# Two-layer attention kernel on one core: a group's scores in two stretches instead of four, the first behind the weighting

## The chip, the cores and the metric

The kernel runs on one core of a Trainium2 chip. A core has five engines with a queue each, which work in order and wait for one another by semaphores: TensorE (PE, with its weight loads as PEld), VectorE (DVE), ScalarE (ACT), GpSimd (POOL) and SyncE (SP), which here only issues DMAs. Matmuls write to PSUM, eight banks of 128 x 512 fp32. The metric is the device time of one execution in microseconds (us); less is better.

## What is computed

The reference has two layers over x of shape 8 x 512 x 256. Layer 1 is, for each of the 8 batches, causal attention with 16 heads of 64 and rotary embedding, beside an 8-bit quantised product; layer 2 (a gated attention and a token-mixing network) is not touched by the change. Cut to what matters:

```python
xn = layernorm(x)                                  # B, S, D = 8, 512, 256
q, k, v = (xn @ W + b for W, b in ((Wq, bq), (Wk, bk), (Wv, bv)))   # 16 heads of 64
q, k = rope(q), rope(k)
scores = where(causal, q @ k.T / 8, -1e9)          # per head, 512 x 512
x = x + softmax(scores) @ v @ Wo + bo + int8_product(xn)
```

All of it is fp32, but for the quantised product.

## The kernel before

**Groups.** The heads of a batch are taken eight at a time, so layer 1 is 16 groups, numbered `at` = 0 to 15 (`last`); `b, g = divmod(at, 2)` gives the batch and its half. A group has two pairs of four heads, 2at and 2at + 1. Its steps, each a function of the kernel:

- `project_qk(pair, which)` (L387): four matmuls (L400; each fp32 matmul shows as two passes in the trace) make queries (`which` 0) or keys (1) of four heads; ScalarE takes them out of PSUM with the bias (L405), and SP sends them off with partitions exchanged (`y`, L407). `project(at, which)` does both pairs.
- `turn_qk(pair, which)` (L410): the rotary embedding, two VectorE products (L417) and one sum on GpSimd (L432).
- `project_v(at)` (L434): the values, taken out by ScalarE (L449) and stored; `load_v` (L455) fetches them back in another layout (`vr`, one buffer).
- `scores(at, run)` (L469): the causal scores in blocks of 32 queries. The 16 blocks are packed into nine units of one pair of PSUM banks each, and the units into five runs (two units each, the fifth has one). Every unit takes two banks; matmuls are 64 rows by 32 columns, eight side by side in the array (L480).
- `soften(at, run)` (L487): VectorE adds the mask, finds the maximum and writes the scores to SBUF (`p`, L508, four buffers), ScalarE exponentiates with the sum (L512).
- `divide(at, run)` (L518): reciprocal on VectorE (L523), multiplication by it on GpSimd (L531), an instruction for each block and half.
- `turn(at, run)` (L539): VectorE transposes the probabilities in 32 x 32 blocks (L551) into `turned`, four tiles with one buffer each.
- `weigh(at)` (L560): probabilities times values, 256 matmul passes of 32 rows by 64 columns (L568) into four banks. Its first matmul reads a tile that all five runs write, `turn(at, 4)` last. `keep_weighed` (L576) takes them out on ScalarE (L582).
- `output_product` and `add_output` (L356, L368; together `finish`): the output projection (L362) and its addition on VectorE (L371).

`look_at(b)` (L291; statistics on VectorE, L152 to L156, and a small power on GpSimd, L157) and `prepare(b)` (L305; normalisation, L171, and the greatest value, L301) make a later batch's input ready, in the groups with `g == 1` and 1 <= b < 6 and in group 2; `transpose_x` (L312) turns it on TensorE in groups with `g == 0`. The groups 12 and 13 also round and clip an input (L190, L196) and add the quantised product of a batch (`add_quantised`, L199).

**Order.** The tile scheduler is switched off (`manual_schedule`, L256), so each engine's queue has exactly the order in which the program calls these functions; the loop at L813 is that order, written by hand. PSUM has one pool of eight banks in rotation (`bank`, L60): a new tile waits for the readers of the tile eight allocations before it. In the loop of group `at`, TensorE's order is scores 0 of `at`, the weighting of `at - 1`, scores 1, the queries of `at + 1`, scores 2, the values of `at + 1`, scores 3 and 4, the output product of `at - 1`, and the keys of `at + 2`.

## Time and profile before

| | |
|---|---|
| median of 3 runs | 941.17 us (938.4 to 942.62) |
| the profiled execution | 939.1 us, its span 937.2 us |
| PE busy | 923.8 us, 99% of the span |
| DVE busy | 787.4 us, 84% |
| ACT busy | 533.0 us, 57% |
| POOL busy | 540.0 us, 58% |
| granted TensorE clock, mean | 0.999 |
| DMA | 105.40 MB, mean 112 GB/s |

The span runs from the first to the last instruction. "Busy" is the time in which an engine works on an instruction. A row of an engine's timeline gives start, length, engine, line, operation, what it writes and reads, the shape, the number of instructions merged, and in brackets the idle time ahead of it with what ended it. The chain that ended last is the work followed back from the last instruction, at each step to what released it or to the instruction ahead of it on its engine. A table of stretches gives, for each stretch of the span, the busy time of PE, PEld, DVE, ACT and POOL with the number of instructions, then the granted clock, the DMA engines' share and GB/s.

### The profile page before, as it was taken

What the parts mean: (1) busy time and instruction counts of PE and PEld (TensorE: products, weight loads), DVE (VectorE), ACT (ScalarE), POOL (GpSimd) and SP (SyncE); (2) the same over time, 40 slices, a digit from 0 to 9 for tenths busy, and PEclk for the clock granted to TensorE, in tenths of its full rate; (3) what the DMA queues carried; (4) which work ended last, traced back from release to release, by engine and by line L of the source; (5) the groups of instructions that cost most, each with busy time, mean ns of one, the idle gap of its engine ahead of it and who ended that gap; (6) DMA issues with size and microseconds to landing.
All of it is one profiled execution on the core that took longest, in us unless ns stands there. A gap on an engine that the chain in (4) does not pass through costs nothing.

```text
span 937.2 us, 27414 instructions
## 1 busy us (share of the span) xinstructions
PE 923.8 (99%) x10491; PEld 600.8 (64%) x10491; DVE 787.4 (84%) x2431; ACT 533.0 (57%) x1488; POOL 540.0 (58%) x688
## 2 busy tenths in 40 slices
PE   9998999999999999999999999999999999999998
PEld 5446565656666575757565656666657777777776
DVE  4998889898799889978997899899899588888854
ACT  3585555656575656474747566555667434445553
POOL 2676765655665757566665756678666424444311
PEclk9999999999999999999999999999999999999999
DMA  7667453525443545263535435453444132211011
GB/s 212 193 166 201 112 128 126 122 80 138 146 105 96 133 136 131 75 159 92 136 91 160 108 98 137 136 145 106 103 114 126 47 101 79 76 57 39 23 34 34
DMA packets 60930, 105.40 MB, mean 112 GB/s; under 512 B 7552, under 2 KB 38272, under 8 KB 60800
## 3 DMA queue, kind: packets, MB, share of 16 engines
q1 hardware_dynamic: 58928, 102.01, 40.1%
q10 hardware_dynamic: 1872, 1.64, 0.7%
q8 instruction: 83, 1.36, 0.6%
q14 instruction: 47, 0.39, 0.1%
HBM read 39.14 MB, written 28.84 MB: 73 GB/s over the span
## 4 chain that ended last, share of the span: by engine, by line
PE 92%; DVE 4%; issue 1%; ACT 1%; POOL 1%; SPq 0%; DMA 0%; DVEq 0%; ACTq 0%; POOLq 0%
PE pq L400 22%; PE av L568 14%; PE sc L480 13%; PE pw L362 12%; PE pv L443 10%; PE po L727 5%; PE pg L689 3%; PE pvv L701 3%; PE pk L674 3%; PE trc L714 1%; PE plr L240 1%; PE c L646 1%; DVE t L551 1%; PE acc L205 1%; DVE p L508 1%
## 5 line engine op out<-in xcount | busy, mean ns | idle before, releaser
L512 ACT ACTIVATE p<-p,nm 128x64 f32<-128x64 f32 (+15 forms) x512 | 259.9, 512 | 123.1 <-DVE nm L508 98.3
L531 POOL TENSOR_SCALAR p<-p,rs 128x512 f32<-128x512 f32 (+4 forms) x504 | 263.3, 543 | 44.0 <-DVE rs L523 41.9
L432 POOL TENSOR_TENSOR h<-h,y 128x1024 f32<-128x1024 f32 x62 | 161.0, 2596 | 188.9 <-DVE y L417 106.6
L508 DVE CUSTOM_DVE_ANT_0 p<-sc,cmask 128x64 f32<-128x64 f32 (+15 forms) x512 | 190.3, 434 | 61.5 <-PE sc L480 61.5
L551 DVE STREAM_TRANSPOSE t<-p 128x256 f32<-128x256 f32 (+3 forms) x640 | 192.1, 366 | 18.2 <-POOL p L531 18.1
L480 PE MATMUL sc<-h,h 64*32 64x416 f32 (+15 forms) x4096 | 138.7, 393 | 1.9 <-POOL h L432 1.2
L568 PE MATMUL av<-t,vr 32*64 32x192 f32 (+15 forms) x4096 | 128.8, 392 | 4.0 <-issue 4.0
L568 PEld LDWEIGHTS av<-t,vr 32*64 32x64 f32 x4096 | 123.2, 131 | 9.1 <-issue 7.8
L480 PEld LDWEIGHTS sc<-h,h 64*32 64x32 f32 x4096 | 78.8, 106 | 76.0 <-issue 56.5
L405 ACT ACTIVATE l<-pq,cs 128x512 f32<-128x512 f32 x128 | 84.7, 683 | 66.8 <-PE pq L400 54.4
L417 DVE TENSOR_TENSOR y<-y,cs 128x1024 f32<-128x1024 f32 x64 | 110.7, 1729 | 5.8 <-DMA y<-l 5.3
L362 PE MATMUL pw<-wo,att 128*128 128x256 f32 x512 | 114.8, 382 | 0.0
L400 PE MATMUL pq<-xnT,wq 128*128 128x512 f32 x256 | 114.6, 599 | 0.2 <-ACT xnT L321 0.2
L443 PE MATMUL pv<-wv,xnT 128*128 128x512 f32 x256 | 114.3, 599 | 0.0
L400 PE MATMUL pq<-xnT,wk 128*128 128x512 f32 x256 | 112.9, 593 | 0.6 <-DVE nm L508 0.6
L362 PEld LDWEIGHTS pw<-wo,att 128*128 128x128 f32 x512 | 95.9, 190 | 18.5 <-issue 6.1
L512 ACT ACTIVATION_READ_ACCUMULATOR p<-p,nm 128x1 f32 x512 | 97.3, 190 | 0.0
L400 PEld LDWEIGHTS pq<-xnT,wk 128*128 128x128 f32 x256 | 48.6, 190 | 56.6 <-issue 54.1
L443 PEld LDWEIGHTS pv<-wv,xnT 128*128 128x128 f32 x256 | 47.3, 190 | 57.9 <-issue 54.1
L417 DVE TENSOR_TENSOR h<-l,cs 128x1024 f32<-128x1024 f32 x64 | 79.5, 1243 | 4.5 <-ACT l L405 4.5
L400 PEld LDWEIGHTS pq<-xnT,wq 128*128 128x128 f32 x256 | 47.2, 190 | 56.0 <-issue 48.8
L582 ACT ACTIVATE att<-av,cs 128x512 f32<-128x512 f32 x64 | 38.7, 688 | 71.4 <-PE av L568 71.4
(113 smaller groups left out, 949.8 us busy)
## 6 DMA issues: line engine op xcount, KB each, us to landing
y<-l SPq DMA_DIRECT2D x256, 128.0 KB, 2.3
va<-v SPq DMA_DIRECT2D x32, 512.0 KB, 3.1
vr<-va SPq DMA_DIRECT2D x64, 256.0 KB, 4.8
x<-in_x SPq DMA_DIRECT2D x15, 512.0 KB, 4.2
xnf<-xnT SPq DMA_DIRECT2D x8, 512.0 KB, 3.3
x1f<-x SPq DMA_DIRECT2D x7, 512.0 KB, 2.7
out<-y SPq DMA_DIRECT2D x14, 256.0 KB, 2.2
cut_wo<-xnf SPq DMA_DIRECT2D x5, 512.0 KB, 4.2
```

Of the source, the lines that this page charges most:

```text
L362: nc.tensor.matmul(pw[:, j, :], atts[at, p][:, tok], wo[:, 4 * (at % NH) + p, :], start=(p == 0), stop=(p == 3),)
L400: nc.tensor.matmul(pb, w[:, g, k, bass.ts(t, P)], xnT[b][:, k, :], start=(k == 0), stop=(k == NK - 1),)
L405: nc.scalar.activation(l[:, t, :], pb, AF.Identity, bias=cs[:, bias : bias + 1])
L417: nc.vector.tensor_tensor(dst, src, table[:, None, :].to_broadcast([P, 2, S]), ALU.mult)
L432: (engine or nc.gpsimd).tensor_tensor(h, h, y, ALU.add)
L443: nc.tensor.matmul(pb.rearrange("p (g n) -> p g n", g=2), xnT[b][:, k, bass.ts(2 * half + j, P)], wqkv[2][:, 2 * g : 2 * g + 2, k, :], sta ...
L480: nc.tensor.matmul(scored[at, i][e][j * Q : j * Q + Q, :], q[rows, j % 2, bass.ts(i, Q)], k[rows, j % 2, :n], start=True, stop=True,)
L508: nc.vector.tensor_tensor_reduce(p[:, e, col : col + n], sc, cmask[:, S - n :], -1.0 / L**0.5, BIG, ALU.add, ALU.min, nm[:, c : c + 1],)
L512: nc.scalar.activation(p[:, e, col : col + n], p[:, e, col : col + n], AF.Exp, bias=nm[:, c : c + 1], scale=-1.0, accum_out=sm[:, c : c + 1],)
L531: nc.gpsimd.tensor_scalar(p, p, rs[:, c : c + 1], 1.0, ALU.mult, ALU.mult)
L551: nc.vector.transpose(turned[at][c][:, :, at_ : at_ + (n - 1) * pitch(c) + 1 : pitch(c), :], p[:, :, c * P : c * P + n * Q].rearrange("p e ...
L568: nc.tensor.matmul(banks[j][e * L : e * L + L, i * Q :], vs[at][rows, m, c, bass.ts(e, L)], t[c][rows, e, m * pitch(c) + m : m * pitch(c) ...
```

## The change

Group 1 is taken out of the loop and written out, with the calls that it had; only `turn(1, 4)`, which the loop of group 2 had made behind its first scores, now stands at the end of group 1. The loop runs from 2. In it:

- the weighting of `at - 1` comes first on TensorE; scores 0 and 1 follow it together, then the queries of both pairs (one ahead of `soften(at, 1)` in the program, one behind the keys' `turn_qk`), then the values, then scores 2, 3 and 4 together, and the output product and keys as before;
- `turn(at, 4)` stands at the end of the group itself, behind `divide(at, 4)` and the output additions;
- `soften` of runs 2 and 3 stand together, `divide` and `turn` of run 2 behind them; `turn_qk` of the second pair's queries is behind `soften(at, 4)`, and the output additions are behind `turn(at, 3)`;
- `look_at` moves up behind the weighting, `prepare` stands behind `turn(at, 1)`.

Behind the loop, group 14 gets its scores of run 2, with their `soften` and `divide`, in the tail. No computation is added or left out.

The diff, with the written-out group 1 cut:

```diff
@@ -810,65 +810,94 @@
         x_next.append(load_x(2))
         turn(0, 3)
         project(2, 1)
-        for at in range(1, last):
+
+        at = 1
+        scores(1, 0)
+        turn(0, 4)
+        soften(1, 0)
+        weigh(0)
+        keep_weighed(0)
...
+        turn(1, 3)
+        project(3, 1)
+        divide(1, 4)
+        turn(1, 4)
+        for at in range(2, last):
             b, g = divmod(at, NH)
             two = at + 2 <= last
+            inputs = g == 1 and 1 <= b < B - 2
+            clips = at in (last - 3, last - 2)
             if g == 0 and b < B - 1:
                 fetch(b)
-            scores(at, 0)
-            turn(at - 1, 4)
-            soften(at, 0)
             if at == last - 3:
                 scale_of_x()
             weigh(at - 1)
+            if inputs:
+                look_at(b + 2)
+            turn_qk(2 * at + 2, 1)
             keep_weighed(at - 1)
-            if at == 1:
-                load_rest()
-                load_second()
-                fetch(0)
-            turn_qk(2 * at + 2, 1)
             load_v(at)
-            if at in (last - 3, last - 2):
+            if clips:
                 s_ = at - last + 3
                 fetch_output(s_, output_tile(f"x1e_{s_}"))
                 xnl = fetch_input(s_, work.tile([P, NK, S], F32, tag="xnl", name=f"xnl_{s_}"))
-            divide(at, 0)
-            turn_qk(2 * at + 3, 1)
             if at == last - 2:
                 first_norm = norm(0, xpool.tile([P, NT, D], F32, tag="x", name="yn_0"))
+            scores(at, 0)
             scores(at, 1)
+            soften(at, 0)
+            project_qk(2 * at + 2, 0)
             soften(at, 1)
-            turn(at, 0)
+            turn_qk(2 * at + 3, 1)
             if at == 2:
                 look_at(2)
             elif at == 4:
                 spread_rest()
                 spread_second()
-            elif g == 1 and 1 <= b < B - 2:
-                look_at(b + 2)
-            divide(at, 1)
+            divide(at, 0)
             if at == last - 1:
                 first_norm()
-            project(at + 1, 0)
-            if at in (last - 3, last - 2):
+            project_qk(2 * at + 3, 0)
+            if clips:
                 round_input(xnl)
-            scores(at, 2)
-            soften(at, 2)
+            turn(at, 0)
+            divide(at, 1)
             turn_qk(2 * at + 2, 0)
             turn(at, 1)
-            if at in (last - 3, last - 2):
+            if at == 2 or inputs:
+                prepare(b + 2 if inputs else 2)
+            if clips:
                 xq = work.tile([P, NK, S], BF16, tag="xq", name=f"xq_{s_}")
                 clip(xnl, xq)
-            divide(at, 2)
-            if at == 2:
-                prepare(2)
-            elif g == 1 and 1 <= b < B - 2:
-                prepare(b + 2)
             if at == last - 1:
                 turn_qk(2 * at + 3, 0)
-            if at == 1:
-                nc.gpsimd.tensor_tensor(bob, bob, rw[:, 2, :], ALU.add)
-                add_biases(0)
             project_v(at + 1)
             if at == last - 1:
                 break
@@ -876,21 +905,27 @@
                 transpose_x(b + 1)
                 if b + 2 < B:
                     x_next.append(load_x(b + 2))
-            scores(at, 3)
+            for run in (2, 3, 4):
+                scores(at, run)
+            soften(at, 2)
             soften(at, 3)
+            divide(at, 2)
+            turn(at, 2)
+            soften(at, 4)
             turn_qk(2 * at + 3, 0)
-            turn(at, 2)
             divide(at, 3)
-            scores(at, 4)
-            soften(at, 4)
-            if at in (last - 3, last - 2):
+            if clips:
                 for half in range(2):
                     add_quantised(s_, half, xq, line(f"u_{s_}_{half}"))
-            finish(at - 1)
+            for half in range(2):
+                output_product(at - 1, half)
             turn(at, 3)
+            divide(at, 4)
+            for half in range(2):
+                add_output(at - 1, half)
+            turn(at, 4)
             if two:
                 project(at + 2, 1)
-            divide(at, 4)
             if g == 0 and b < B - 1:
                 add_biases(b)
             if at == last - 4:
@@ -898,9 +933,11 @@
 
 
         at = last
-        scores(at - 1, 3)
-        soften(at - 1, 3)
+        for run in (2, 3):
+            scores(at - 1, run)
+            soften(at - 1, run)
         nc.sync.dma_start(w2, second.rearrange("j (k p) n -> p j k n", p=P))
+        divide(at - 1, 2)
         turn(at - 1, 2)
         divide(at - 1, 3)
         scores(at - 1, 4)
```

More of the change, by code (lines that the diff above doesn't have):

```diff
@@ L812, in two_layers @@
         project(2, 1)
-        for at in range(1, last):
+        at = 1
[4 more added lines that the diff above has]
+        keep_weighed(0)
+        load_rest()
+        load_second()
+        fetch(0)
+        turn_qk(4, 1)
+        load_v(1)
+        divide(1, 0)
+        turn_qk(5, 1)
+        scores(1, 1)
+        soften(1, 1)
+        turn(1, 0)
+        divide(1, 1)
+        project(2, 0)
+        scores(1, 2)
+        soften(1, 2)
+        turn_qk(4, 0)
+        turn(1, 1)
+        divide(1, 2)
+        nc.gpsimd.tensor_tensor(bob, bob, rw[:, 2, :], ALU.add)
+        add_biases(0)
+        project_v(2)
+        scores(1, 3)
+        soften(1, 3)
+        turn_qk(5, 0)
+        turn(1, 2)
+        divide(1, 3)
+        scores(1, 4)
+        soften(1, 4)
+        finish(0)
+        turn(1, 3)
[3 more added lines that the diff above has]
+        for at in range(2, last):
             b, g = divmod(at, NH)
             two = at + 2 <= last
+            inputs = g == 1 and 1 <= b < B - 2
+            clips = at in (last - 3, last - 2)
             if g == 0 and b < B - 1:
                 fetch(b)
-            scores(at, 0)
-            turn(at - 1, 4)
-            soften(at, 0)
             if at == last - 3:
```

## The prediction, made before the result was known

> **What bounds the kernel now.** I read four views in this order: the page's busy shares, the chain that ended last, a table of stretches, and the rows of single engines. The chain over one group of layer 1 (at = 9: columns start, length, what, count):

> ```profile
> 434.19 1.89 PE sc L480 x45
> 436.07 7.95 PE av L568 x163
> 444.02 2.05 PE sc L480 x57
> 446.07 7.06 PE pq L400 x16
> 453.13 1.94 PE sc L480 x64
> 455.07 7.06 PE pv L443 x16
> 462.14 2.32 PE sc L480 x80
> 464.45 7.11 PE pw L362 x32
> 471.56 6.87 PE pq L400 x16
> 478.43 1.89 PE sc L480 x45
> ```

> Nothing but TensorE stands on it: weighting to weighting takes 44.2 us without a gap. The next view, two whole groups (an even one, at = 4, and an odd one, at = 5), shows how far the others are from being the bound:

> ```profile
> 211.40:256.66 45.26, 45.26 (x603) 28.61 (x605) 37.21 (x129) 27.37 (x82) 29.13 (x40) 1.00 0.52 141
> 256.66:300.89 44.23, 44.23 (x594) 27.68 (x597) 41.13 (x138) 26.17 (x80) 27.62 (x37) 1.00 0.39 97
> ```

> After the length stand PE, PEld, DVE, ACT and POOL. VectorE has 8 us free in the even group and 3 us in the odd one, where it normalises a later batch's input. So PE is the bound, with VectorE close behind. The last view is where they meet: the weighting of a group reads `turned`, and `turn(at, 4)` (L551) is its last writer. Rows of VectorE and GpSimd at the end of at = 8, and the first softening of at = 9:

> ```profile
> 431.72 0.93 POOL L531 TENSOR_SCALAR p<-p,rs 128x256 f32<-128x256 f32 x2 [1.08 <-DVE rs L523]
> 432.68 0.77 DVE L551 STREAM_TRANSPOSE t<-p 128x256 f32<-128x256 f32 x2 [1.06 <-POOL p L531]
> 435.30 0.69 DVE L508 CUSTOM_DVE_ANT_0 p<-sc,cmask 128x512 f32<-128x512 f32 x1 [1.85 <-PE sc L480]
> ```

> The last turn starts at 432.68 and the weighting at 436.07: some 3 us to spare. In group 1 the same turn (118.29) was late, and the weighting stood still until 118.84, 0.55 after the turn's start. The softening starts 1.2 us after its scores do (434.12 in PE's rows) and 0.8 us *before* the weighting. That lead is what the change gives up.

> **What the change does to PE.** The order becomes av, sc0, sc1, pq, pq, pv, sc2, sc3, sc4, pw, pw, pk. No matmul is added. Changes of tile shape fall from 8 to 5. Price: the same 16 passes take 7.06 us behind scores and 6.87 behind `pw`, so 0.2 us a change, 0.6 us a group. [...] With PE unhindered a group would take 43.6.

> **The new chain, walked from rows.** Take 0 as the start of weigh(at-1). PE: weighting to 7.95, sc0 to 9.85, sc1 to 11.9, queries to 18.9, values to 25.9, sc2 from there. VectorE first turns the keys of 2at+2 (two L417 of 1.13 = 2.3), hidden beside the weighting; in the odd groups look_at (1.75, L152 to L156) hides there too. Then it idles until the first scores: their first softening starts 1.2 after the stretch (435.30 less 434.12, 445.16 less 443.95), so at 9.15.
> - soften 0 (435.30 to 437.91 = 2.6) to 11.8; soften 1 (445.16 to 447.92 = 2.76) to 14.5; turn_qk of 2at+3 keys 2.27 to 16.8; reciprocals 0.15.
> - POOL's queue holds that pair's sum (L432, 2.35) ahead of divide 0 (L531, 4.14): 16.8 to 19.15 to 23.3. ScalarE's exponentials (3.4, behind keep_weighed's 2.4) end at 13.9 and are not late. turn 0 can end only 0.7 behind its divide, at 24.0: VectorE waits 4.3 of these 7.
> - turn_qk of the queries to 26.4, while POOL runs divide 1. There POOL loses 2 us:

> ```profile
> 643.97 5.67 POOL L531 TENSOR_SCALAR p<-p,rs 128x384 f32<-128x384 f32 x8 [1.54 <-DVE rs L523]
> 651.95 3.64 POOL L531 TENSOR_SCALAR p<-p,rs 128x320 f32<-128x320 f32 x8
> ```

> The first of these had two L417 beside it (646.63, 647.87), the second none. So divide 1 ends at 29.85 and turn 1 at 30.5 (1.3 of waiting).
> - sc2 was readable at 27.1, so VectorE is 3.4 late already. soften 2 to 33.3, soften 3 to 36.0, reciprocal, divide 2 (3.65) to 39.85, turn 2 to 40.3 (1.4 waited), soften 4 (0.66) to 41.0, turn_qk 2.27 to 43.3.
> - POOL's sum of that turn_qk stands ahead of divide 3 in its queue: 45.6, then 3.65 to 49.25; turn 3 to 49.65 (3.5 waited). add_output twice 1.2, with divide 4 beside it; turn 4 starts at 50.95; weighting 0.55 later, at **51.5**.

> PE meanwhile: sc4 takes the banks of sc2's first pair (eight banks for ten tiles) and waits for soften 2 until 31.9, `pw` for its second pair until 33.3; then 14 us of `pw` and `pk` end at 47.4, and PE idles 4.1 us. So the wait that is removed, none, is replaced by one for `turn(at, 4)`.

> **Other edits.** prepare (L171, L301: 1.98 + 1.14 = 3.1) of the odd groups lies ahead of soften 2: 54.6. Group 2 has its look_at's small power on POOL (1.0) ahead of divide 0 as well: 55.6. The greatest-value step ahead of weigh(11) (0.4 VectorE, 0.33 transpose, latencies): 1.2. Groups 12 and 13: clip 1.1 ahead of soften 2, round_input a little, and add_quantised's 2.5 on POOL ahead of divide 4, of which 1.8 shows: 54.5. Group 1, written out, keeps its instructions: nothing. Queues: the queries' `y` transfers (L407) leave SP after load_v, some 16 to 22, land 2.3 us later and are read at 24 and 41; `vr` lands before 15: nothing, with 2 to 10 us of cover each.

> **Sum.** Before, by starts of the weighting: odd 44.25, even 45.5, group 2 48.3, 12 46.1, 13 45.0.
> Even 4, 6, 8, 10: 4 x 6.0 = 24. Odd 3, 5, 7, 9: 4 x 10.35 = 41. Group 11: 11.3. Group 2: 7.3. Groups 12 and 13: 8.4 + 9.5. Group 14 walked the same way reaches weigh(14) at about 51 instead of 42.7 (661.72 to 704.45): 8. Together 110 us. The profiled execution took 939.1 (span 937.2 and 1.9 around it); the median shown is 941.2, 2 us above. 939 + 110 = 1049, near **1050**.

> **What no row shows.** How PE's clock takes an idle of 4 us in every group. The largest gap on PE in the trace is 2.31 us (70.3 to 72.6) and kept the full clock; behind the last matmul, after 2.3 us, it fell:

> ```profile
> 933.50:935.80 2.30, 0.06 (x1) 0.00 (x0) 0.88 (x2) 0.00 (x0) 0.00 (x0) 1.00 0.30 99
> 935.80:937.20 1.40, 0.00 (x0) 0.00 (x0) 0.00 (x0) 0.00 (x0) 0.00 (x0) 0.51 0.08 25
> ```

> (The eighth figure is the granted clock.) At the start, 26 warm-up passes of 128 columns took 5.83 us, 0.22 each, against 0.13 for the eight of `pxt` after them: it took 5.6 us to reach full speed. So a gap costs between nothing and half of 5.6 = 2.8 us, on the weighting, which is on the chain: 0 to 36 us over 13 groups. I take nothing, since the nearest gap on this program's path (2.31) lost nothing, and keep the upper end for the range. [...]

> **Rivals.**
> 1. *The gain.* PE stays the bound and 13 groups save 0.6 each: 939 - 8 = 931. It needs everything between readable sc2 (27.1) and the next weighting's PE slot (43.6) to fit into 16.5 us. VectorE's own durations there add up to 16.0 (5.5 softening, 2.8, 0.7, 2.3, 2.8, 1.2, 0.55, reciprocals), so all of POOL's waits and the lateness of 3.4 would have to vanish. 0.05; between the two, no change: 0.03.
> 2. *Half the waits.* The walk contains 10.5 us of waiting for POOL in a group (4.3, 1.3, 1.4, 3.5); without any, VectorE's queue alone would give 41 (even) and 44 (odd), about PE's own time. If half of it is covered, even groups take 46.2 and odd 49.3: 4 x 0.7 + 5 x 5 + some 12 for groups 2 and 12 to 14 = 40, 979. Against it: the waits come from queue order, which the rows follow instruction by instruction. 0.17.
> 3. *The clock falls.* Forecast plus half of 36: 1067, up to 1085. For: the drop at 935.8. 0.25.
> Forecast: 0.50, by itself 1030 to 1065.

> **Numbers.** The range 1000 to 1085 holds the forecast, the clock and the upper part of half the waits. Under 0.5% (4.7 us, about what a measurement can tell from no change) counts as the same. Slower 0.92, same 0.03, faster 0.05.

> **What would show it.** Right: starts of the weighting 51 to 52 apart in even groups and 54 to 55 in odd; about 4 us of PE idle ahead of `av`, ended by L551; VectorE idle some 6 us in the weighting (even groups); L512 no worse; divide 1 over 5 us; PE's share near 88%. Clock: `av` over 9 us with a granted clock under 1. Wrong: the weighting starts right behind `pk`, or VectorE's waits for L531 under 5 us a group.

## The result and the profile after

| | before | after |
|---|---|---|
| median | 940.5 us (4 runs, 938.4 to 942.6) | 1082.3 us (4 runs, 1082.1 to 1084.6) |
| span of the profiled execution | 937.2 us | 1080.4 us |
| PE busy | 99% | 89% |
| VectorE busy | 84% | 72% |

The ratio is 1.151, with a 95% interval of 1.148 to 1.154. The forecast was slower, 1050 us, with a range of 1000 to 1085.

The first lines to read are the page's shares and PE's clock in 40 slices (`PEclk`, in tenths of full speed). Busy time of PE is 38 us longer for the same number of instructions, and the clock, with a mean of 0.948, has dents all through layer 1:

```profile
PE 961.8 (89%) x10491; PEld 633.2 (59%) x10491; DVE 783.2 (72%) x2431; ACT 532.1 (49%) x1488; POOL 539.1 (50%) x688
...
PEclk9999988999898989898989998998988999999999
...
PE 61%; DVE 20%; issue 10%; POOL 7%; ACT 1%; DMA 0%; DVEq 0%; POOLq 0%; ACTq 0%
```

The last line is the chain that ended last: PE had 92% of it before, now VectorE and GpSimd hold 27%. Where PE waits (engine, line, what for: us in total, times, longest):

```profile
PE av L568 <- issue: 51.0, 13, 4.9
PE sc L480 <- DVE nm L508: 47.1, 12, 5.9
```

The weighting stands still 13 times ("issue" means that no single event in the profile shows its end; the rows below do), and scores 4 wait 12 times for a bank that soften 2 has to read first. Before, the weighting stood still 4 times, 4.0 us in all, and scores never for a softening. The chain over group 6, an even one (columns start, length, what, count):

```profile
345.59 8.05 PE av L568 x157
353.64 1.13 PE sc L480 x16
...
360.19 1.14 DVE h L417
361.33 1.13 DVE y L417
362.60 2.36 POOL h L432
364.95 1.35 POOL p L531 x2
366.32 1.88 DVE t L551 x6
...
371.88 2.39 POOL p L531 x5
374.30 0.68 DVE t L551 x2
...
378.42 7.14 PE pw L362 x32
385.56 6.88 PE pq L400 x16
392.44 4.86 issue
```

Where before only PE stood, the work now goes from the weighting through the first scores to VectorE (softening), to GpSimd (a sum, then a divide) and back to VectorE. In its last lines the view follows PE up to the 4.86 us that it can put down to nothing. What ends them is seen in the rows of the other engines at the end of the same group, VectorE's first, then GpSimd's:

```profile
388.74 0.23 DVE L523 RECIPROCAL rs<-sm 128x4 f32<-128x4 f32 x2
392.30 1.48 DVE L551 STREAM_TRANSPOSE t<-p 128x256 f32<-128x256 f32 x5 [3.33 <-POOL p L531]
394.06 1.56 DVE L551 STREAM_TRANSPOSE t<-p 128x256 f32<-128x256 f32 x5 [0.28 <-POOL p L531]
395.54 0.12 DVE L523 RECIPROCAL rs<-sm 128x2 f32<-128x2 f32 x1
395.58 1.26 DVE L371 TENSOR_TENSOR x<-pw,x 128x512 f32<-128x512 f32 x2
396.77 0.76 DVE L551 STREAM_TRANSPOSE t<-p 128x256 f32<-128x256 f32 x2
```

```profile
388.91 2.35 POOL L432 TENSOR_TENSOR h<-h,y 128x1024 f32<-128x1024 f32 x1 [3.79 <-DVE rs L523]
391.23 3.65 POOL L531 TENSOR_SCALAR p<-p,rs 128x320 f32<-128x320 f32 x8
```

VectorE has its reciprocals at 388.9; GpSimd could divide at once, but the embedding's sum is ahead of it in its queue until 391.2, so turn 3 waits 3.3 us. The last turn starts at 396.77, and the weighting 0.53 later, at 397.30. PE's keys had ended at 392.4. In all the groups 2 to 13 but group 11, the weighting starts 0.53 to 0.55 us after the start of the last turn, and at least 2.7 us after the end of the keys: it is the last turn that it waits for.

Time went here: from weigh(1) to weigh(14) 726.9 us instead of 585.5, which is 141 of the 143 us of span. What stands ahead of group 2 and behind group 14 changed by 2.

### The profile page after: what moved, and what is told of

It reads as the page before. It is cut to its first block, busy times and chain, and to the rows that moved or that the text cites. A ratio compares the mean times of both kernels' runs of the same rounds, so it can differ in the third digit from the quotient of the medians.

```text
span 1080.4 us, 27388 instructions
## 1 busy us (share of the span) xinstructions
PE 961.8 (89%) x10491; PEld 633.2 (59%) x10491; DVE 783.2 (72%) x2431; ACT 532.1 (49%) x1488; POOL 539.1 (50%) x688
## 4 chain that ended last, share of the span: by engine, by line
PE 61%; DVE 20%; issue 10%; POOL 7%; ACT 1%; DMA 0%; DVEq 0%; POOLq 0%; ACTq 0%
PE av L568 14%; PE pq L400 12%; PE pw L362 10%; DVE p L508 8%; DVE t L551 5%; PE sc L480 5%; POOL p L531 5%; PE po L727 5%; PE pv L443 3%; PE pg L689 3%; PE pvv L701 3%; POOL h L432 2%; PE pk L674 2%; DVE y L417 2%; DVE h L417 1%
## 5 line engine op out<-in xcount | busy, mean ns | idle before, releaser
L531 POOL TENSOR_SCALAR p<-p,rs 128x512 f32<-128x512 f32 (+4 forms) x504 | 271.1, 558 | 120.5 <-DVE rs L523 120.0
L512 ACT ACTIVATE p<-p,nm 128x64 f32<-128x64 f32 (+15 forms) x512 | 259.5, 512 | 122.1 <-DVE nm L508 122.1
L551 DVE STREAM_TRANSPOSE t<-p 128x256 f32<-128x256 f32 (+3 forms) x640 | 197.8, 371 | 127.1 <-POOL p L531 127.0
L432 POOL TENSOR_TENSOR h<-h,y 128x1024 f32<-128x1024 f32 x62 | 148.0, 2387 | 269.4 <-DVE rs L523 185.0
L508 DVE CUSTOM_DVE_ANT_0 p<-sc,cmask 128x64 f32<-128x64 f32 (+15 forms) x512 | 188.2, 434 | 87.4 <-PE sc L480 87.4
L568 PE MATMUL av<-t,vr 32*64 32x416 f32 (+15 forms) x4096 | 150.2, 441 | 51.7 <-issue 51.0
L480 PE MATMUL sc<-h,h 64*32 64x64 f32 (+15 forms) x4096 | 141.9, 402 | 47.1 <-DVE nm L508 47.1
L568 PEld LDWEIGHTS av<-t,vr 32*64 32x64 f32 x4096 | 138.3, 146 | 72.5 <-issue 68.9
L480 PEld LDWEIGHTS sc<-h,h 64*32 64x32 f32 x4096 | 86.4, 107 | 99.6 <-issue 78.5
L362 PE MATMUL pw<-wo,att 128*128 128x256 f32 x512 | 125.6, 407 | 2.1 <-DVE nm L508 1.9
L362 PEld LDWEIGHTS pw<-wo,att 128*128 128x128 f32 x512 | 104.1, 207 | 26.5 <-PE sc L480 8.5
L400 PE MATMUL pq<-xnT,wq 128*128 128x512 f32 x256 | 114.6, 599 | 0.2 <-ACT xnT L321 0.2
L400 PE MATMUL pq<-xnT,wk 128*128 128x512 f32 x256 | 112.9, 592 | 1.0 <-DVE nm L508 1.0
L443 PE MATMUL pv<-wv,xnT 128*128 128x512 f32 x256 | 112.9, 593 | 0.0
L512 ACT ACTIVATION_READ_ACCUMULATOR p<-p,nm 128x1 f32 x512 | 97.7, 191 | 0.0
L417 DVE TENSOR_TENSOR y<-y,cs 128x1024 f32<-128x1024 f32 x64 | 82.6, 1290 | 16.1 <-DMA y<-l 15.0
L417 DVE TENSOR_TENSOR h<-l,cs 128x1024 f32<-128x1024 f32 x64 | 82.0, 1282 | 4.3 <-ACT l L405 4.3
L443 PEld LDWEIGHTS pv<-wv,xnT 128*128 128x128 f32 x256 | 48.4, 190 | 60.8 <-issue 60.2
L400 PEld LDWEIGHTS pq<-xnT,wk 128*128 128x128 f32 x256 | 48.6, 190 | 57.0 <-issue 53.6
L400 PEld LDWEIGHTS pq<-xnT,wq 128*128 128x128 f32 x256 | 47.2, 190 | 56.0 <-issue 49.5
```

The lines of the kernel that those rows point to most:

```text
L362: nc.tensor.matmul(pw[:, j, :], atts[at, p][:, tok], wo[:, 4 * (at % NH) + p, :], start=(p == 0), stop=(p == 3),)
L400: nc.tensor.matmul(pb, w[:, g, k, bass.ts(t, P)], xnT[b][:, k, :], start=(k == 0), stop=(k == NK - 1),)
L417: nc.vector.tensor_tensor(dst, src, table[:, None, :].to_broadcast([P, 2, S]), ALU.mult)
L432: (engine or nc.gpsimd).tensor_tensor(h, h, y, ALU.add)
L443: nc.tensor.matmul(pb.rearrange("p (g n) -> p g n", g=2), xnT[b][:, k, bass.ts(2 * half + j, P)], wqkv[2][:, 2 * g : 2 * g + 2, k, :], sta ...
L480: nc.tensor.matmul(scored[at, i][e][j * Q : j * Q + Q, :], q[rows, j % 2, bass.ts(i, Q)], k[rows, j % 2, :n], start=True, stop=True,)
```

## The experiments

Four theories were open after the result: (a) a queue of VectorE and GpSimd work that no longer fits beside PE, to which both moves add; (b) the first move alone; (c) the second alone; (d) how much of it is PE's clock. Where a comparison has no interval, it is one run beside the runs of the kernel before on the same chip (median 938.8 in the first set, 939.5 in the second).

**The first move alone.** In the kernel before, from group 2 on (this and the edits below are cut to what they do):

```diff
-            scores(at, 0); turn(at - 1, 4); soften(at, 0)      # ahead of weigh(at - 1)
+            scores(at, 0); scores(at, 1); soften(at, 0); soften(at, 1); divide(at, 0)   # behind both turn_qk of keys
+            turn(at, 4)                                         # end of the group
```

> The kernel before, with only the first stretch moved: scores 0 stand behind the weighting, directly ahead of scores 1, their softening ahead of softening 1, and turn(at, 4) ends the group itself; scores 2 and scores 3 and 4 stay where they were. Theory (a queue of VectorE and GpSimd work has to fit between readable scores and the next weighting, and the two moves share one slack): walked from rows, the last turn is ready 42.7 us after the weighting's start in even groups and 44.6 in odd ones, so PE stays the bound or nearly: 935 to 946 us. Rival (the place of the first scores alone makes the loss): VectorE idles 6 us in each weighting and every group loses about that: 1000 to 1030 us.

Measured: 962.4 us, ratio 1.027 (1.023 to 1.031). Even groups take 45.1 to 46.5 us, as PE alone would (the 46.5 has a weighting of 9.5 us, behind 2.6 us of idle); groups 3, 5, 7 and 9 take 46.8 instead of 44.25, with PE idle 2.6 us ahead of the weighting behind them. So the lead of the first softening is missed in these odd groups, where VectorE also prepares an input. They make 10 of the 24 us; groups 2 and 11 to 14 make another 12, which was not followed. The walk had 44.6 there: it took prepare at 3.1 us and not at the 4.1 that it needs beside GpSimd's divide and sum (L171 2.90, L301 1.22), and let turn 3 end with its divide, where softening 4, the additions and its own ten transposes come after turn 2. (b) falls as the whole cause: it makes 24 of 143 us.

**The second move alone.** Scores 2, 3 and 4 together in the kernel before, with the order behind them that the change has:

```diff
-            scores(at, 2); soften(at, 2)          # ahead of the values
+            for run in (2, 3, 4): scores(at, run)          # behind the values
+            soften(at, 2); soften(at, 3); divide(at, 2); turn(at, 2); soften(at, 4)
+            turn_qk(2 * at + 3, 0); divide(at, 3); ...; turn(at, 3); divide(at, 4)
```

> The kernel before, with only the second stretch: scores 2, 3 and 4 together behind the values, with the changed kernel's order of softening, dividing and turning behind them; scores 0 and their softening stay ahead of the weighting. Theory: soften 2 and 3, divide 2, turn 2, turn_qk, divide 3, turn 3 stand one behind the other from sc2 (25.3 us after the weighting's start) and end at about 46.5 in even and 48 in odd groups: 965 to 985 us. Rival (the first move makes the whole loss): as before, 936 to 946. Rival (the second stretch makes the whole loss): over 1040.

Measured: 1005.9 us. Even groups take 47.7 to 49.1 (some 46.5 walked), odd ones 51.2 to 51.8 (48). Part of the rest is a transfer: VectorE's L417 waits 49.6 us in all for `y`, 5.3 before, and 3.5 to 4.9 in the odd groups 3 to 9; in this order it wants `y` of the queries sooner than they land. So (c) is also a part: 67 us. The two alone sum to 91, both together cost 143. That fits (a): each by itself first uses up the slack that PE's work left. Slower weightings do not explain the difference: over 8.05 us each, weightings 1 to 13 take 3.9 and 13.9 us more in the two alone, 19.5 in both.

**The lead given back.** The changed kernel, with the first scores again ahead of the weighting:

```diff
+            scores(at, 0); soften(at, 0)
             weigh(at - 1)
...
+            divide(at, 0)                          # behind load_v and the first turn_qk
             scores(at, 1)
```

> The changed kernel with scores 0 and their softening ahead of the weighting again, and divide 0 behind the first turn_qk; all else as changed. Theory: turn 0 no longer waits for divide 0, and everything behind it comes about 6.4 us earlier; even groups about 45.3 us, odd 49, the weighting at full clock in most groups: 975 to 1000 us. Rival (the second stretch alone makes the loss): above 1060.

Measured: 1013.7, so 69 us come back, less than the 82 to 107 expected. Groups 3 to 10 take 47.7 to 51.8 us, most of them 49.2 to 49.6: the waits behind the second stretch stay (turn 3 still waits 3.3 us in group 7). The weightings were expected at full clock in most groups; the 13 of them still take 12 us over 8.05 each, and the mean granted clock is 0.978.

**The clock.** The changed kernel with a filler on PE:

```diff
-                for k in range(NK):
+                for k in list(range(NK)) * 2:      # keys of the second pair, groups 2 to 13
```

> The changed kernel with the key projections of the second pair made twice in groups 2 to 13 (the same result into the same bank, four more matmuls, 3.4 us of PE in a group), so that PE is idle for 1 to 1.5 us instead of 4.9 ahead of the weighting. It adds work that the reference doesn't need. Theory (the idle halves the clock in the first microseconds of the weighting): every weighting takes 8.05 us instead of up to 10.8, odd groups 55.5: about 1062 us, less though PE has 41 us more to do. Rival (the long weightings come from something else, transfers or a shared port): weightings stay at 10 us, 1082 or above.

Measured: 1066.3, so 16 us *less* with 41 us more of PE work, and a mean granted clock of 0.973 instead of 0.948. The long weightings are gone where the filler closed the gap: weigh(3) to weigh(10) take 7.9 to 8.6 us, where weigh(4), (6), (8) and (10) had taken 10.0 to 10.8. Two, weigh(2) and weigh(11), still take 9.9 us, with 1.1 us of idle inside, which was not followed. The rival, transfers at that time, falls on the changed kernel's own rows: weigh(1) takes 8.05 us, at a granted clock of 1.00, although the DMA engines are busy 86% of its first 4.4 us, with 211 GB/s, and weigh(13) takes 10.33 us, at 0.50 in its first 4.4 us, with the DMA engines idle in them. What the long weightings are made of is seen in a table of stretches of that kernel around one gap (the eighth figure is the granted clock):

```profile
283.22:288.08 4.86, 0.00 (x1) 0.03 (x1) 4.58 (x15) 0.69 (x1) 3.98 (x9) 0.76 0.00 0
288.08:292.50 4.42, 4.42 (x59) 3.57 (x67) 3.24 (x11) 0.00 (x0) 4.04 (x5) 0.50 0.88 271
292.50:298.10 5.60, 5.60 (x216) 5.51 (x207) 1.23 (x1) 0.02 (x1) 2.36 (x1) 1.00 0.31 73
```

PE idles for 4.86 us, the clock falls inside the gap and stays at half for the first 4.4 us of the weighting, in which 59 matmul passes start; the 5.6 us after them start 216. So (d) is some 16 to 20 of the 143 us.

**GpSimd's queue.** The changed kernel with one call moved:

```diff
+            turn_qk(2 * at + 3, 0)                 # ahead of project_v, soften 2
...
             soften(at, 4)
-            turn_qk(2 * at + 3, 0)
             divide(at, 3)
```

> The changed kernel with one call moved: turn_qk of the second pair's queries stands ahead of soften 2 (behind turn 1 and prepare) instead of behind soften 4, so that GpSimd's sum is not ahead of divide 3 in its queue. Theory: turn 3's wait of 3.3 us goes, VectorE's 2.3 move earlier and pay some 1 us in even groups beside the sum of the first pair; even groups about 49.5 us, odd about 54.7, the half clock as before: about 1050 us. Rival (the waits for GpSimd are covered and only the lost lead counts): no difference, 1078 to 1086.

Measured: 1054.4, 28 us less (32 expected): the waits of turns for L531 fall from 127 to 101 us in all. The even groups did not gain (51.5 to 53.4), because soften 2 comes later, scores 4 wait 4.7 us for its bank, the granted clock is 0.85 from 366 to 376 us and 0.81 in the next 10, `pw` takes 8.7 us instead of 7.1, and PE reaches the next weighting no sooner. PE's rows in group 6:

```profile
375.33 1.31 PE L480 MATMUL sc<-h,h 64*32 64x256 f32 x16 [4.74 <-DVE nm L508]
376.67 8.72 PE L362 MATMUL pw<-wo,att 128*128 128x256 f32 x32
385.23 7.03 PE L400 MATMUL pq<-xnT,wk 128*128 128x512 f32 x16
392.19 1.11 PE L568 MATMUL av<-t,vr 32*64 32x512 f32 x16
```

A stall that went gave way to another one. Groups 3, 5, 7 and 9 take 54.1 to 55.8 us, near the 54.7 walked, but that is luck. In group 5 the last turn starts 52.6 us after weigh(4) instead of 57.0, and 2.2 of these 4.4 us are weigh(4) itself (7.87 instead of 10.02); PE, with 9.4 us for `pw`, gets to the weighting only at 54.9. So the 28 us are the queue and the clock together, and this run does not part them.

**Prepare moved.** The changed kernel, preparing inputs where VectorE idles:

```diff
             turn_qk(2 * at + 2, 1)
+            if g == 0 and 2 <= b < B - 2: prepare(b + 1)
...
-            if at == 2 or inputs: prepare(b + 2 if inputs else 2)
+            if at in (2, last - 4): prepare(b + 2 if inputs else 2)
```

> The changed kernel with prepare of groups 3, 5, 7 and 9 moved into the weighting of the next (even) group, behind its first turn_qk, where VectorE idles. Theory: each of the four odd groups loses 3.8 us and the even ones gain none: 1065 to 1068 us, with the half clock unchanged. Rival (VectorE's idle in the weighting is no idle, or prepare is hidden already): 1080 to 1086.

Measured: 1062.9, 19.5 less. Groups 3, 5, 7 and 9 take 53.5 to 54.5 us instead of 57.5 to 58.3. These four make 16 of the 19.5, 4.0 each, so VectorE's idle in the weighting was real, and prepare was fully on the chain. Group 13, whose weighting took 7.9 us here instead of 10.3, makes another 2.4.

**The second stretch with repairs.** The second move alone, with `turn_qk` of the second queries ahead of soften 2 and prepare in the next group:

> The second stretch alone (scores 0 ahead of the weighting), with the two repairs: turn_qk of the second pair's queries ahead of soften 2, and prepare of groups 3, 5, 7 and 9 in the next group behind divide 1. Theory: the last turn is ready 43 us after the weighting's start in even and odd groups, ahead of PE, so PE is the bound again and has two changes of tile shape fewer: 0.1 to 0.2 us each, 3 to 5 us in 13 groups; groups 12 and 13, with the clip and the quantised product, may lose 1 us: 934 to 940 us, against 938.8 before. Rival (scores 2, 3 and 4 together always bring the queue behind PE): 960 or more.

Measured: 965.4, ratio 1.028 (1.026 to 1.030): a miss. Groups 4 and 6 take 44.8, 0.4 us under before, but groups 3, 5, 7 and 9 take 46.3 to 47.3, group 11, which kept its prepare, 50.1 instead of 44.5, and groups 12 and 13 lose 1.9 and 3.5. The chain of group 9 names a wait that the expectation had left out:

```profile
457.89 1.15 ACT l L405 x2
459.10 0.51 SPq L407
...
463.46 2.38 DMA y<-l
...
468.03 2.55 DVE h L417
470.58 1.14 DVE y L417
```

ScalarE takes the queries out of PSUM behind its exponentials, SP issues the eight transfers one after the other, at 0.5 to 0.6 us each, the second embedding's first product takes 2.6 us instead of 1.2 (in the kernel before such a product takes 1.2 us with GpSimd idle, and 2.3 on average, up to 3.4, with GpSimd's sum beside it), and soften 2 starts 4.7 us after its stretch of scores, where 1.2 is usual. Scores 4 then wait for the bank (14.3 us in all).

**Scores 2 early.** The other way to two stretches: the kernel before with one call moved, on PE's queue alone:

```diff
+            scores(at, 2)
             project(at + 1, 0)
...
-            scores(at, 2)
             soften(at, 2)
```

> The kernel before with one call moved on PE's queue alone: scores 2 directly behind scores 1, ahead of the queries; the order of every other engine stays. Two stretches of scores too, and two changes of tile shape fewer, but scores 2 come earlier for VectorE instead of later. Theory: PE stays the bound and gains 0.3 us in 14 groups: 933 to 937 us. Rival (a change of tile shape costs nothing that the next matmuls don't hide): 938 to 940. Rival (values wait for the banks of scores 2): slower by up to 1 us a group.

Measured: 933.5 us, ratio 0.994 (0.992 to 0.997): it beats both kernels, the one before by a small but clear 0.6%. The chain is PE's again:

```profile
256.00 7.28 PE av L568 x158
263.28 3.81 PE sc L480 x103
267.09 7.06 PE pq L400 x16
274.15 6.87 PE pv L443 x16
281.02 2.32 PE sc L480 x80
283.34 7.10 PE pw L362 x32
290.44 6.87 PE pq L400 x16
297.31 1.89 PE sc L480 x44
```

Groups 3, 5, 7 and 9 take 43.86 us instead of 44.25, and 4 and 6 44.74 instead of 45.1 to 45.3: some 0.4 us for two changes of tile shape.

## Why the prediction was right, and what it mis-sized

**The mechanism held, step by step.** Us after the start of weigh(at - 1):

| | walked | group 6 | group 5 (odd) |
|---|---|---|---|
| soften 0 starts | 9.15 | 9.2 | 11.1 |
| soften 1 ends | 14.5 | 14.5 | 16.5 |
| turn 0 ends | 24.0 | 23.5 | 25.4 |
| turn 1 ends | 30.5 | 30.1 | 32.1 |
| soften 3 ends | 36.0 (odd 39.1) | 35.6 | 41.4 |
| turn 2 ends | 40.3 (43.4) | 40.2 | 46.0 |
| turn 3 ends | 49.65 (52.8) | 49.95 | 55.75 |
| next weighting | 51.5 (54.6) | 51.7 | 57.5 |

Group 6, with its weighting at full clock (8.05 us, granted 1.00), was walked to 0.2 us at its end and to 0.5 on the way. The waits came out near what was walked: 3.7 at turn 0 (4.3), 1.3 at turn 1 (1.3), 1.6 at turn 2 (1.4), 3.6 at turn 3 (3.5). Divide 1 took 5.64 beside the two products (5.65 taken), and PE's share is 89% (88). The experiments show the parts: both moves cost, and GpSimd's queue order and prepare were on the chain. The rival in which half the waits are covered (979) and the gain (931) fall. So does the forecast by itself, 1030 to 1065: the time lies in the part of the range that the third rival, "The clock falls", had added.

**The mis-sized term is the clock.** Under "What no row shows" the prediction took nothing, "since the nearest gap on this program's path (2.31) lost nothing". The two rows of the span's end, which it showed, spoke against that: there 2.3 us of idle were enough to lose it. And that the gap of 2.31 was free did not carry over: the gap of 2.32 at the same place in the changed kernel lost the clock (last section). The expected idle was 4.1 us, and the gaps became 4.9 behind most even groups and 2.8 to 3.2 behind the odd groups 3 to 9. The weightings 1 to 13 together took 19.5 us more than 8.05 each, and closing the gaps brought 16. The third rival, up to 1085, is what happened.

**The rest.** Of 33 us over the walked sum, the clock is 19.5. A longer weighting counts in full: group 8, whose weighting took 1.6 us more than group 6's, took 1.6 more. prepare took 3.8 and not 3.1 (its L171 2.6, beside GpSimd's sum): 4 us in six groups. Group 2 took 3.2 longer than walked, of which prepare explains 0.7. In group 11 the greatest-value step put the weighting 1.44 us behind the start of the last turn instead of 0.53: 0.9, where 1.2 was taken. Outside the groups came 2. What is left, 2.5 in group 2 and some 5 over the others, 1.2 each in groups 12 and 13, was not followed.

That the range held is in part luck. Its upper end, 1085, was the walked sum and 36 us for the clock alone. The clock took 19.5, and 13 us that no term of the range stood for took most of the rest.

**The gain on PE** (0.2 us a change of tile shape) was sized rightly, but was behind the chain and so worth nothing in the changed kernel. It is seen where PE is the bound again: in scores2_early, and in groups 4 and 6 of second_mended, 0.4 us each.

## What to carry to other kernels

When one engine is busy all the time, the others' order around it is what keeps it so: before moving its work, walk the queue of the engines behind it from the first result to the last one that it needs back, with their waits, and compare that with the work PE has left in between. Here, moving PE's work *earlier* than its readers need it (scores 2 behind scores 1) kept their order and took the saving, 6 us; moving it later, and the first scores behind the weighting, spent the same slack twice, 143 us. A stall on PE has a second price where it loses the clock (19.5 us here), and a few matmuls that only fill the gap can be cheaper than the gap (41 us of them saved 16).

## What the hardware showed that was not expected

In the profile of the changed kernel, the 17 idles of PE of 3.53 us or more in layer 1 all overlapped a stretch of half clock or were followed by one, for 3.41 or 6.83 us. Of the six from 2.3 to 3.25 us, two were (2.32 and 3.24) and four were not (2.53, 2.75, 3.01, 3.21). The gap ahead of weigh(0) is in both kernels. In the kernel before it is 2.31 us long, and the clock stayed full; in the changed kernel it is 2.32 us long, and 3.41 us of half clock followed.

```profile
68.83:72.24 3.41, 1.43 (x48) 0.55 (x32) 2.95 (x11) 1.64 (x3) 2.14 (x5) 1.00 0.93 263
72.24:75.66 3.42, 3.09 (x85) 3.12 (x91) 3.42 (x15) 2.18 (x7) 0.00 (x0) 1.00 0.80 192
```

```profile
70.68:74.09 3.41, 1.37 (x26) 1.40 (x34) 3.41 (x14) 0.46 (x1) 0.43 (x1) 1.00 0.92 264
74.09:77.50 3.41, 3.41 (x75) 3.41 (x66) 3.41 (x12) 3.03 (x12) 0.00 (x0) 0.50 0.74 133
```

Over both profiles, with the trace's ends of matmuls, 553 steps have the full clock. The 19 with 2.04 us of idle or more were all followed by half clock, the 532 with less than 1.85 by full clock; of the two between, the one with 1.91 (changed) was followed by half clock, the one with 1.99 (before) by full. Of the 33 steps at half clock, the 19 in which PE idled 0.42 us or less were followed by the full clock, the 14 with 0.62 or more by another at half. So a gap of 2.3 us cost 1.6 us in one kernel (weigh(0) took 9.65 us instead of 8.05) and nothing in the other, by where it fell.
